# Splitting the gate matmuls of a fused LSTM and mixture-of-experts kernel: f, g and i first, o of both halves last

## The chip, the cores and the metric

The kernel runs on one core of one Trainium2 chip. The metric is the device time of one execution in microseconds (us). The time before is the median of three runs, 2253.83 us (2253.7 to 2257.63).

## What is computed

The input `x` has N = 2 sequences of T = 1024 steps with D = 256 features; all data are 32-bit floats. An LSTM with 256 units runs over the steps, from a given first hidden state and a zero cell state:

```python
def step(carry, xw_t):
    prev_h, prev_c = carry
    a = xw_t + prev_h @ Wh                   # Wh: 256 x 1024, xw = x @ Wx + b
    i = jax.nn.sigmoid(a[:, :Hdim])
    f = jax.nn.sigmoid(a[:, Hdim:2 * Hdim])
    o = jax.nn.sigmoid(a[:, 2 * Hdim:3 * Hdim])
    g = jnp.tanh(a[:, 3 * Hdim:])
    next_c = f * prev_c + i * g
    next_h = o * jnp.tanh(next_c)
    return ((next_h, next_c), next_h)
```

Its outputs are added to `x`. A mixture of experts follows on each token: two shared experts (SiLU-gated, 512 wide), and of eight routed experts (GELU, 256 wide) the two with the best scores, weighted by gates. Their scaled sum is added again.

## The kernel before

Each step needs the hidden state of the step before, so the 1,024 steps run one after the other (the loop over `t`). The experts of tokens that are done are cut into small units and put between the steps.

**The recurrent product.** The 256 units are kept as two halves `m` (K = 2), the 256 inputs of the product as two halves `k`. The stationary operand is a window of 32 columns of the stored hidden states (`h_window`): two of them hold the current step, the others are zero, so that eight steps (TH) of one group of gates can gather in the same PSUM tile, each in rows of its own. The moving operand is 64 columns of `wh_sb`: a pair of gates of 32 units. Four such products, `q` = 0 to 3, write the four groups of 32 PSUM partitions of `ps[m]`. `BLOCKS` lists the order of the eight blocks (k, m, pair) of four products in a step. The first three need only half 0 of h, the other five need half 1. A product of 32-bit floats is two weight loads and two matmuls in the profile (all on line 255, in `product`).

**The cell update.** For each half VectorE transposes `ps[m]` (128x64) in blocks of 32x32 within the same PSUM bank (line 787). ScalarE takes the sigmoids of i, f and o (line 790, 6 elements per partition) and the tanh of g (line 791, 2 elements). VectorE multiplies f by the old cell state (line 794), copies g into `seen` (line 798), and a scan over four elements (line 799) makes i * g + f * c for both sequences; its factors are zeros, which `results` fills beforehand by two ScalarE copies per 16 steps (line 697), and i. ScalarE takes the tanh of the cell state (line 807), VectorE multiplies by o and writes the new h (line 810). The order on VectorE is: both transposes; forget, copy and scan of half 0; the same of half 1; both h.

**Around it.** The products of `x` with `Wx` are made in blocks of 128 steps and kept with their bias by ScalarE (`keep_inputs`, line 613). `inject` puts them into the gate tile of the next eight steps by matmuls with the identity, at least one product per step. `Fill` holds queues of units of expert work for TensorE, ScalarE and VectorE; each step takes from them what its due time asks for, for TensorE at most two full products (ROOM), or, when nothing is due, one idle product with the identity.

The order of instructions is that of the program text. The code counts TensorE's instructions, four per product (`fill.issued`), and a table `WAITS` of steps with an additional one. Where the count would reach a multiple of 256 (FETCH) within the first 16 instructions (EARLY) of the next step, it injects one product more or cuts an injection into pieces:

```python
count = next(
    (n for n in range(max(0, t % TH + 1 - put), left + 1)
     if -(fill.issued + 4 * n) % FETCH > EARLY), left)
first = -(fill.issued + 4 * count) % FETCH
for i in range(count):
    more = i == count - 1 and first <= EARLY
    inject(nxt, t // TH + 1, put, 2 + first // 4 if more else 1)
    put += 1
```

Of the kernel before, what the change touches and what calls it, by code (L numbers as in the profile page):

```python
# [16 lines left out]
P = 128  # L17
N = 2
# [3 lines left out]
Q = 4  # L22
# [26 lines left out]
FETCH = 256  # L49
EARLY = 16  # L50
WAITS = (
    1, 8, 16, 24, 32, 40, 48, 56, 64, 72, 80, 88, 96, 104, 112, 120, 128, 136, 144, 149,
    152, 157, 160, 160, 165, 168, 176, 181, 184, 189, 192, 197, 200, 208, 216, 224, 232,
    240, 248, 256, 264, 272, 280, 288, 296, 304, 312, 320, 328, 336, 344, 352, 360, 368,
    376, 384, 392, 400, 408, 416, 419, 421, 423, 424, 428, 430, 432, 435, 437, 439, 440,
    440, 447, 448, 456, 464, 472, 480, 488, 496, 504, 512, 520, 528, 529, 536, 544, 552,
    560, 568, 576, 584, 592, 600, 608, 616, 624, 632, 640, 648, 656, 664, 672, 680, 688,
    688, 696, 704, 712, 720, 728, 736, 744, 752, 760, 768, 776, 784, 792, 800, 808, 816,
    824, 832, 840, 848, 856, 864, 872, 880, 888, 896, 904, 912, 920, 928, 930, 933, 935,
    936, 940, 942, 944, 947, 949, 951, 952, 956, 958, 960, 963, 965, 968, 976, 984, 992,  # L60
    999, 1000, 1004, 1006, 1008, 1011, 1013,
)
ISSUED = -188
# [4 lines left out]

BLOCKS = [
    (0, 0, 0), (0, 0, 1), (0, 1, 0), (1, 0, 0), (1, 0, 1), (0, 1, 1), (1, 1, 0), (1, 1, 1)  # L70
]


class Fill:
# [6 lines left out]
    def __init__(self):  # L81
        self.pe, self.act, self.dve = deque(), deque(), deque()
        self.aside = deque()
        self.last = False
        self.issued = ISSUED
        self.step = 0
        self.banks = FILL_BANKS
# [47 lines left out]
def lstm_moe_kernel(  # L135
# [89 lines left out]
    zero = const.tile([P, TB, K, N], F32, name="zero")  # L225
    nc.vector.memset(zero, 0.0)
# [20 lines left out]
    stepsp = ctx.enter_context(tc.tile_pool(name="steps", bufs=2))  # L247
# [5 lines left out]
    def product(*operands, **how):  # L253
        fill.issued += 4
        nc.tensor.matmul(*operands, **how)  # L255
# [348 lines left out]
    blocks = {}  # L604
    made = set()

    def pairs(blk):
        flat = blocks[blk].rearrange("p (h c) w -> p h (c w)", c=2)
        return flat.rearrange("p h (g c r) -> p h g c r", c=2, r=PAIR)

    def keep_inputs(blk, tile_, w0, w1, ps):
        h, c = divmod(tile_, 2)
        nc.scalar.activation(  # L613
            pairs(blk)[:, h, w0 // PAIR : w1 // PAIR, c, :],
            ps[:, : w1 - w0].rearrange("p (g r) -> p g r", r=PAIR),
            AF.Identity, bias=b_sb[:, tile_ : tile_ + 1],
        )
        made.update((blk, tile_, w) for w in range(w0, w1, PAIR))
# [12 lines left out]
    def queue_inputs(blk, w0=0):  # L631

        if w0 == 0:
            blocks[blk] = inputs.tile([P, 2 * Q, N * XB], F32, name="inputs")
        st = {}

        def unit(i, j):
            if j == 0:
                st["ps"] = bank()
            ps = st["ps"]  # L640
            input_product(blk, 2 * i + j // K, j % K, w0, N * XB, ps[:, j // K])
            if j == 2 * K - 1:
                fill.to_act(0.5, lambda: keep_inputs(blk, 2 * i, w0, N * XB, ps[:, 0]))
                fill.to_act(0.5, lambda: last(2 * i + 1, ps))

        def last(tile_, ps):
            keep_inputs(blk, tile_, w0, N * XB, ps[:, 1])
            fill.let_go()

        fill.pe.extend(  # L650
            (int(j == 0), 2, lambda i=i, j=j: unit(i, j)) for i in range(Q) for j in range(2 * K)
        )

    def inject(banks, grp, i, pieces=1):
        m, q = divmod(i, Q)
        blk, g = divmod(grp, XB // TH)
        assert all((blk, 4 * m + 2 * (q // 2) + c, g * PAIR) in made for c in range(2))
        for piece in range(pieces):
            w0, w1 = 64 * piece // pieces, 64 * (piece + 1) // pieces
            product(  # L660
                banks[m][0][q * ROWS : (q + 1) * ROWS, w0:w1],
                pairs(blk)[:, 2 * m + q // 2, g].rearrange("p c r -> p (c r)"),
                ident[:, q % 2 * 64 + w0 : q % 2 * 64 + w1],
                start=(piece == 0), stop=False, skip_group_check=True,
            )

    def gates_tile(m):

        a = gates_ps.tile([P, 4, P], F32, name=f"ps{m}")
        return a[:, 0, :64], a[:, 1, :64], a[:, 2:]  # L670
# [21 lines left out]
    def results():  # L692
        flat = stepsp.tile([P, TB, K, 8 * N], F32, name="results")
        sgm = flat[:, :, :, : 6 * N].rearrange("p u m (a n z) -> p u m a n z", n=N, z=2)
        gf = flat[:, :, :, 6 * N :].rearrange("p u m (n z) -> p u m n z", z=2)
        for m in range(K):
            nc.scalar.activation(sgm[:, :, m, 0, :, 0], zero[:, :, m], AF.Copy)
        return sgm, gf


    nc.scalar.activation(stepp.tile([P, N], F32, name="seen0"), zero[:, 0, 0], AF.Sigmoid)
    nxt_results = results()

    cells = [cells_ps.tile([P, 3, N, 2], F32, name=f"c{m}") for m in range(K)]
    c_prev = [cells[m][:, 1] for m in range(K)]
    for m in range(K):
        nc.vector.memset(cells[m], 0.0)
# [3 lines left out]
    nxt = [gates_tile(m) for m in range(K)]  # L711
# [6 lines left out]
    blocks[0] = inputs.tile([P, 2 * Q, N * XB], F32, name="inputs")  # L718
# [6 lines left out]
    for i in range(K * Q):  # L725
        inject(nxt, 0, i)
    due = 12
    for t in range(T):
        fill.step = t
        grp, u = divmod(t, TB)  # L730
        if t % TH == 0:
            cur, nxt = nxt, [gates_tile(m) for m in range(K)]
            ps, turned, busy = [a[0] for a in cur], [a[1] for a in cur], nxt[0][2]
            spare = False
        if u == 0:
            sgm, gf = nxt_results
# [9 lines left out]
        for k, m, pair in BLOCKS:  # L746
            for q in range(Q):
                w0 = q * D + m * P + pair * 64
                product(
                    ps[m][q * ROWS : (q + 1) * ROWS],  # L750
                    h_window(t, k, pair),
                    wh_sb[:, k, w0 : w0 + 64],
                    start=False,
                    stop=(t % TH == TH - 1 and k == K - 1 and pair == 1),
                    skip_group_check=True,
                )
        left = max(1, due - t)
        done = fill.run_pe(-(-len(fill.pe) // left), ROOM)
        if t % TH == 0:
            spare = not done  # L760
        if spare and not done:
            product(
                busy, ident, ident.unsqueeze(1).to_broadcast([P, 2, P]),
                start=(t % TH == 0), stop=False, skip_group_check=True,
            )

        if t // TH + 1 < T // TH:
            put = put if t % TH else 0
            fill.issued += WAITS.count(t)

            left = K * Q - put
            count = next(
                (n for n in range(max(0, t % TH + 1 - put), left + 1)
                 if -(fill.issued + 4 * n) % FETCH > EARLY), left)
            first = -(fill.issued + 4 * count) % FETCH
            for i in range(count):
                more = i == count - 1 and first <= EARLY
                inject(nxt, t // TH + 1, put, 2 + first // 4 if more else 1)
                put += 1

        rows = slice(N * (t % TH), N * (t % TH + 1))
        gates = [turned[m].rearrange("p (a r) -> p a r", r=PAIR)[:, :, rows] for m in range(K)]
        c_new = [cells[m][:, t % 2] for m in range(K)]
        seen = [stepp.tile([P, N], F32, name=f"seen{m}") for m in range(K)]
# [4 lines left out]
        def squash(m):  # L789
            nc.scalar.activation(sgm[:, u, m, :, :, 1], gates[m][:, 0:3], AF.Sigmoid)  # L790
            nc.scalar.activation(gf[:, u, m, :, 0], gates[m][:, 3], AF.Tanh)  # L791

        def forget(m):
            nc.vector.tensor_mul(gf[:, u, m, :, 1], sgm[:, u, m, 2, :, 1], c_prev[m][:, :, 1])  # L794

        def cell(m):

            nc.vector.tensor_copy(seen[m], gf[:, u, m, :, 0])  # L798
            nc.vector.tensor_tensor_scan(  # L799
                c_new[m].rearrange("p n z -> p (n z)"),  # L800
                sgm[:, u, m, 0].rearrange("p n z -> p (n z)"),
                gf[:, u, m].rearrange("p n z -> p (n z)"),
                0.0, ALU.mult, ALU.add,
            )

        def squash_cell(m):
            nc.scalar.activation(cells[m][:, 2, :, 0], c_new[m][:, :, 1], AF.Tanh)  # L807

        def output(m):
            nc.vector.tensor_mul(h_cols(t + 1)[:, m], sgm[:, u, m, 1, :, 1], cells[m][:, 2, :, 0])  # L810
# [4 lines left out]
        for m in range(K):  # L815
            forget(m)
            cell(m)
            squash_cell(m)
        for m in range(K):
            output(m)  # L820
        if u == TB // 2 and t + TB < T:
            nxt_results = results()
        else:
            fill.run(fill.act, 1.0)
        c_prev = c_new
# [102 lines left out]
```

## Time and profile before

| | |
|---|---|
| Runs: median, lowest, highest | 2253.83, 2253.7, 2257.63 us |
| Profiled execution, and its span | 2254.8 us, 2254.8 us |
| Granted TensorE clock, mean over the span | 0.996 |
| Busy: TensorE, its weight loads, VectorE, ScalarE | 2033.5, 1484.8, 1571.3, 909.5 us |
| Recurrent matmuls (line 255, 128x64) | 65536, mean 221 ns |
| Transposes (line 787) | 2048, mean 265 ns |
| Sigmoids of i, f, o (line 790) and tanh of g (line 791) | 2048 each, mean 176 and 167 ns |
| Forget product, copy, scan (lines 794, 798, 799) | 2048 each, mean 156, 162, 175 ns |
| Tanh of the cell (line 807), new h (line 810) | 2048 each, mean 157 and 153 ns |

PE is TensorE's matmul side, PEld its weight loads, DVE is VectorE, ACT ScalarE, SP the engine that issues most DMAs. Matmul records overlap, so the busy time of PE is no measure of how much of the array works. In a timeline the columns are start, duration, engine, line, operation, result <- operands, shape and number of instructions merged; in brackets stands the engine's idle time before, and what ended it. "issue" there means that the engine waited for nothing that the profile shows.

### The profile page before, as it was taken

The numbers are of one execution on the slowest core, as the hardware profiler recorded it, in microseconds if no ns is written. First come the engines' busy times: TensorE is split into PE (matmuls) and PEld (weight loads), VectorE is DVE, ScalarE is ACT, GpSimd is POOL, SyncE is SP. The second block draws the span as 40 slices with busy tenths as digits, with TensorE's granted clock in tenths as the row PEclk, the third lists the DMA queues.
The fourth block names the chain that finished last, engine by engine and source line by source line (L and its number), as shares of the span: only waits on it lengthen the run. The fifth ranks groups of instructions, "written<-read, shape, count | busy, mean of one in ns | idle before, by whom it ended". The sixth has DMA issues, their size and how long they took to land.

```text
span 2254.8 us, 159246 instructions
## 1 busy us (share of the span) xinstructions
PE 2033.5 (90%) x70612; PEld 1484.8 (66%) x70612; DVE 1571.3 (70%) x11041; ACT 909.5 (40%) x6487; POOL 2.7 (0%) x9
## 2 busy tenths in 40 slices
PE   8988899888989889998798899988898988989998
PEld 6666666666666666777666666666666666667787
DVE  5666667776777667777667767676676776667776
ACT  3334344433444334443344443444434344334443
POOL 0000000000000000000000000000000000000000
PEclk9999999999999999999999999999999999999999
DMA  2111100000000000000000000000000000000000
GB/s 65 35 35 35 35 28 5 5 5 7 7 5 5 5 7 7 5 7 7 5 6 5 5 5 7 7 4 5 5 7 7 4 5 5 7 7 5 5 9 7
DMA packets 15330, 23.84 MB, mean 11 GB/s; under 512 B 2864, under 2 KB 14128, under 8 KB 14640
## 3 DMA queue, kind: packets, MB, share of 16 engines
q1 hardware_dynamic: 14352, 12.62, 1.9%
q8 instruction: 552, 9.04, 1.7%
q14 instruction: 138, 1.13, 0.2%
q10 hardware_dynamic: 288, 1.05, 0.1%
HBM read 11.56 MB, written 2.10 MB: 6 GB/s over the span
## 4 chain that ended last, share of the span: by engine, by line
PE 61%; DVE 36%; issue 3%; DMA 0%; SPq 0%; ACT 0%
PE ps L255 53%; DVE ps L787 10%; DVE c L799 10%; PE ps_f L255 8%; DVE results L794 7%; DVE seen L798 6%; DVE h L810 3%; DMA wh_sb<-in_wh_dram 0%; SPq L165 0%; DVE acc L534 0%; SPq L173 0%; SPq L171 0%; SPq L170 0%; DVE acc L492 0%; ACT y L542 0%
## 5 line engine op out<-in xcount | busy, mean ns | idle before, releaser
L255 PE MATMUL ps<-wh_sb,h 128*32 128x64 f32 x65536 | 1143.8, 221 | 214.3 <-DVE h L810 210.5
L255 PEld LDWEIGHTS ps<-wh_sb,h 128*32 128x32 f32 x65536 | 975.1, 110 | 393.1 <-DVE h L810 386.8
L787 DVE STREAM_TRANSPOSE ps<-ps 128x64 f32<-128x64 f32 x2048 | 543.4, 265 | 498.5 <-PE ps L255 426.0
L790 ACT ACTIVATE results<-ps 128x6 f32<-128x6 f32 x2048 | 361.3, 176 | 1103.8 <-DVE ps L787 1009.4
L810 DVE TENSOR_TENSOR h<-results,c 128x2 f32<-128x2 f32 x2048 | 314.2, 153 | 168.4 <-ACT c L807 168.2
L807 ACT ACTIVATE c<-c 128x2 f32<-128x2 f32 x2048 | 321.5, 157 | 217.5 <-DVE c L799 181.7
L799 DVE TENSOR_TENSOR_SCAN c<-results 128x4 f32<-128x4 f32 x2048 | 358.2, 175 | 0.0
L791 ACT ACTIVATE results<-ps 128x2 f32<-128x2 f32 x2048 | 342.4, 167 | 0.0
L798 DVE COPY seen<-results 128x2 f32<-128x2 f32 x2048 | 332.8, 162 | 0.0
L794 DVE TENSOR_TENSOR results<-results,c 128x2 f32<-128x2 f32 x2048 | 319.3, 156 | 0.0
L255 PEld LDWEIGHTS ps<-ident,inputs 128*32 128x32 f32 x2090 | 124.0, 108 | 265.7 <-issue 228.4
L255 PE MATMUL ps<-ident,inputs 128*32 128x64 f32 (+2 forms) x2090 | 263.9, 230 | 0.3
L255 PE MATMUL ps_f<-x2T,w_sb 128*128 128x256 f32 (+3 forms) x640 | 173.4, 379 | 0.0
L255 PE MATMUL ps_f<-x2T,r_sb 128*128 128x256 f32 (+3 forms) x640 | 173.2, 378 | 0.0
L255 PE MATMUL ps_f<-r_sb,h_r 128*128 128x256 f32 (+1 forms) x520 | 165.9, 419 | 0.9 <-DVE acc L492 0.9
L255 PEld LDWEIGHTS ps_f<-x2T,r_sb 128*128 128x128 f32 (+1 forms) x640 | 88.5, 184 | 22.8
L255 PEld LDWEIGHTS ps_f<-x2T,w_sb 128*128 128x128 f32 (+1 forms) x640 | 86.7, 184 | 21.8 <-issue 0.2
L255 PEld LDWEIGHTS ps_f<-r_sb,h_r 128*128 128x128 f32 (+1 forms) x520 | 80.0, 184 | 23.3 <-DVE acc L492 1.3
L255 PE MATMUL ps_f<-xT_sb,wx_sb 128*128 128x256 f32 (+2 forms) x384 | 84.5, 346 | 0.3 <-ACT inputs L613 0.3
L255 PE MATMUL ps<-ident 128*128 128x256 f32 x232 | 82.8, 443 | 1.4 <-POOL ident masks.py:199 1.4
L255 PE MATMUL ps_f<-w_sb,h_s 128*128 128x256 f32 (+1 forms) x256 | 82.6, 419 | 0.0
L492 DVE SCALAR_TENSOR_TENSOR acc<-ps_f,gate,acc 128x256 f32<-128x256 f32 (+1 forms) x128 | 61.1, 478 | 1.2 <-PE ps_f L255 1.0
(87 smaller groups left out, 475.1 us busy)
## 6 DMA issues: line engine op xcount, KB each, us to landing
r_sb<-in_r_w1T_dram SPq DMA_DIRECT2D x16, 128.0 KB, 2.5
r_sb<-in_r_w2T_dram SPq DMA_DIRECT2D x16, 128.0 KB, 2.1
out_dram<-acc SPq DMA_DIRECT2D x15, 128.0 KB, 2.1
xT_sb<-in_xT_dram SPq DMA_DIRECT2D x14, 128.0 KB, 2.5
wx_sb<-in_wx_dram ACTq DMA_DIRECT2D x2, 512.0 KB, 4.3
wh_sb<-in_wh_dram SPq DMA_DIRECT2D x2, 512.0 KB, 6.2
w_sb<-in_s_w1T_dram SPq DMA_DIRECT2D x8, 128.0 KB, 2.2
w_sb<-in_s_w3T_dram SPq DMA_DIRECT2D x8, 128.0 KB, 2.2
```

The costliest lines, as they stand in the source:

```text
L255: nc.tensor.matmul(*operands, **how)
L492: nc.vector.scalar_tensor_tensor(acc, ps, st["gate"][:, i, e : e + 1], acc, ALU.mult, ALU.add)
L787: nc.vector.transpose(turned[m], ps[m])
L790: nc.scalar.activation(sgm[:, u, m, :, :, 1], gates[m][:, 0:3], AF.Sigmoid)
L791: nc.scalar.activation(gf[:, u, m, :, 0], gates[m][:, 3], AF.Tanh)
L794: nc.vector.tensor_mul(gf[:, u, m, :, 1], sgm[:, u, m, 2, :, 1], c_prev[m][:, :, 1])
L798: nc.vector.tensor_copy(seen[m], gf[:, u, m, :, 0])
L799: nc.vector.tensor_tensor_scan(c_new[m].rearrange("p n z -> p (n z)"), sgm[:, u, m, 0].rearrange("p n z -> p (n z)"), gf[:, u, m].rearrang ...
L807: nc.scalar.activation(cells[m][:, 2, :, 0], c_new[m][:, :, 1], AF.Tanh)
L810: nc.vector.tensor_mul(h_cols(t + 1)[:, m], sgm[:, u, m, 1, :, 1], cells[m][:, 2, :, 0])
```

## The change

The four gates get a new order in the weights, f, g, i, o, and each half's products are cut differently. Per half and input half there are now three kinds of blocks: f and g together (64 columns), i alone (32 columns) and o alone (32 columns). The o blocks of both halves go last and into one tile of its own, `out_gate`, in another PSUM bank; it is reused by every group of eight steps. A step has 12 blocks of four products instead of eight.

```diff
+FG, IN, OUT = (0, 0, 64), (1, 64, 96), (None, 96, 128)
 BLOCKS = [
-    (0, 0, 0), (0, 0, 1), (0, 1, 0), (1, 0, 0), (1, 0, 1), (0, 1, 1), (1, 1, 0), (1, 1, 1)
+    (0, 0, FG), (0, 0, IN), (0, 1, IN),
+    (1, 0, FG), (1, 0, IN), (0, 1, FG), (1, 1, FG), (1, 1, IN),
+    (0, 0, OUT), (0, 1, OUT), (1, 0, OUT), (1, 1, OUT),
 ]
+ORDER = [1, 3, 0, 2]
+PUT = [0, 0, 2, 4, 5, 6, 7, 8, 8]
...
-        for k, m, pair in BLOCKS:
+        for i, (k, m, (pair, a, b)) in enumerate(BLOCKS):
+            into = ps[K if pair is None else m]
             for q in range(Q):
-                w0 = q * D + m * P + pair * 64
+                w0 = q * D + m * P
                 product(
-                    ps[m][q * ROWS : (q + 1) * ROWS],
-                    h_window(t, k, pair),
-                    wh_sb[:, k, w0 : w0 + 64],
+                    into[q * ROWS : (q + 1) * ROWS, : b - a],
+                    h_window(t, k, m if pair is None else pair),
+                    wh_sb[:, k, w0 + a : w0 + b],
```

The sigmoid is taken as a tanh of half the argument: the weights, inputs and bias of g are doubled once (on the chip), one tanh with a scale of 0.5 covers f, g and i of a half, and the missing (1 + ...) / 2 are put into the forget product and the scan. The scan has eight elements, four per sequence, with constants set once; the copies into `seen` and the fills of `results` go. The o gates of both halves get one 128x32 transpose and one sigmoid.

```diff
         def squash(m):
-            nc.scalar.activation(sgm[:, u, m, :, :, 1], gates[m][:, 0:3], AF.Sigmoid)
-            nc.scalar.activation(gf[:, u, m, :, 0], gates[m][:, 3], AF.Tanh)
+            at = bass.AP(
+                tensor=res.tensor,
+                offset=res[:, t % SLOTS, m, 0:1].offset,
+                ap=[res.ap[0], [9, 3], [4, N]],
+            )
+            nc.scalar.activation(at, gates[m][:, 0:3], AF.Tanh, scale=0.5)
+
+        def squash_out():
+            nc.scalar.activation(into[:, :, 0:N, 1], gates[K], AF.Sigmoid)

         def forget(m):
-            nc.vector.tensor_mul(gf[:, u, m, :, 1], sgm[:, u, m, 2, :, 1], c_prev[m][:, :, 1])
+            nc.vector.scalar_tensor_tensor(
+                into[:, m, N : 2 * N, 2], into[:, m, 0:N, 0], 1.0, c_old[m][:, :, 3],
+                ALU.add, ALU.mult,
+            )

         def cell(m):
-            nc.vector.tensor_copy(seen[m], gf[:, u, m, :, 0])
             nc.vector.tensor_tensor_scan(
                 c_new[m].rearrange("p n z -> p (n z)"),
-                sgm[:, u, m, 0].rearrange("p n z -> p (n z)"),
-                gf[:, u, m].rearrange("p n z -> p (n z)"),
-                0.0, ALU.mult, ALU.add,
+                own[:, m, 2], own[:, m, 1], 0.0, ALU.mult, ALU.add,
             )
...
-        for m in range(K):
-            forget(m)
-            cell(m)
-            squash_cell(m)
+        forget(0)
+        transpose(K)
+        squash_out()
+        cell(0)
+        squash_cell(0)
+        forget(1)
+        cell(1)
+        squash_cell(1)
         for m in range(K):
             output(m)
-        if u == TB // 2 and t + TB < T:
-            nxt_results = results()
-        else:
-            fill.run(fill.act, 1.0)
-        c_prev = c_new
+        if t % TH == TH - 1 and t + 1 < T:
+            for q in range(Q):
+                inject(nxt, t // TH + 1, K * Q + q)
+        if t % TH == 3:
+            nc.scalar.activation(stepp.tile([P, N], F32, name="seen"), outs[0], AF.Copy)
+        fill.run(fill.act, 1.0)
```

The injections of f, g and i follow the fixed list `PUT`, without a count of TensorE's instructions: `FETCH`, `EARLY`, `WAITS` and the pieces are gone. The four injections of o come at the end of each eighth step. The kept inputs of o have a tile of their own, so a pair of input tiles takes three ScalarE passes instead of two. The next pair of gate tiles is opened one step later than before.

```diff
         if t // TH + 1 < T // TH:
-            put = put if t % TH else 0
-            fill.issued += WAITS.count(t)
...
-                inject(nxt, t // TH + 1, put, 2 + first // 4 if more else 1)
-                put += 1
+            for i in range(PUT[t % TH], PUT[t % TH + 1]):
+                inject(nxt, t // TH + 1, i)
```

## The prediction, made before the changed kernel ran

> **What bounds the kernel now.** I read the head of the page, its DMA queues and its chain of waits first, then the timeline of one step engine by engine, then TensorE's weight loads around a stall.
>
> ```profile
> span 2254.8 us, 159246 instructions
> PE 2033.5 (90%) x70612; PEld 1484.8 (66%) x70612; DVE 1571.3 (70%) x11041; ACT 909.5 (40%) x6487; POOL 2.7 (0%) x9
> ...
> q8 instruction: 552, 9.04, 1.7%
> ...
> PE 61%; DVE 36%; issue 3%; DMA 0%; SPq 0%; ACT 0%
> ```
>
> The 90% of PE does not mean a full array: a matmul record lasts about 220 ns and overlaps its neighbours. The 70,612 matmul and 70,612 weight-load records are what I need later. The timeline of one step (start, duration, instruction, count; VectorE lines, then ScalarE lines) shows a ring of dependencies:
>
> ```profile
> 1001.16 0.16 DVE L810 TENSOR_TENSOR h<-results,c 128x2 f32<-128x2 f32 x1 [0.16 <-ACT c L807]
> ...
> 1001.89 0.60 DVE L787 STREAM_TRANSPOSE ps<-ps 128x64 f32<-128x64 f32 x2 [0.17 <-PE ps L255]
> ...
> 1002.73 0.16 DVE L794 TENSOR_TENSOR results<-results,c 128x2 f32<-128x2 f32 x1
> 1002.80 0.16 DVE L798 COPY seen<-results 128x2 f32<-128x2 f32 x1
> 1002.92 0.17 DVE L799 TENSOR_TENSOR_SCAN c<-results 128x4 f32<-128x4 f32 x1
> ...
> 1003.32 0.16 DVE L810 TENSOR_TENSOR h<-results,c 128x2 f32<-128x2 f32 x1 [0.17 <-ACT c L807]
> ```
>
> ```profile
> 1002.18 0.18 ACT L790 ACTIVATE results<-ps 128x6 f32<-128x6 f32 x1 [1.05 <-DVE ps L787]
> ...
> 1002.52 0.18 ACT L790 ACTIVATE results<-ps 128x6 f32<-128x6 f32 x1
> ...
> 1003.13 0.16 ACT L807 ACTIVATE c<-c 128x2 f32<-128x2 f32 x1 [0.18 <-DVE c L799]
> ```
>
> The second h of a step (1001.16) releases the matmuls that need it; the second transpose follows 1.06 us later, its gates' sigmoid 0.30 after that, the forget product 0.21, the scan 0.19, the tanh 0.21, the next h 0.19: 2.16 us. Over all 1,023 steps the median from h to h is 2.154 us, with no, one or two filling products alike. 1,023 x 2.154 = 2203.5, plus 11.6 us to the first such h and 20.8 us after the last, is 2236; the other 18.7 us are steps that run over, nearly all of them between h and the second transpose, in TensorE's part.
>
> Most of those overruns have one look. TensorE's weight loads:
>
> ```profile
> 1095.93 0.14 PEld L255 LDWEIGHTS ps<-ident,inputs 128*32 128x32 f32 x3 [0.26 <-issue]
> 1096.29 0.94 PEld L255 LDWEIGHTS ps<-wh_sb,h 128*32 128x32 f32 x64 [0.22 <-DVE h L810]
> 1097.32 0.30 PEld L255 LDWEIGHTS ps_f<-x2T,r_sb 128*128 128x128 f32 x2
> 1098.44 0.92 PEld L255 LDWEIGHTS ps<-wh_sb,h 128*32 128x32 f32 x59 [0.83 <-DVE h L810]
> 1099.67 0.15 PEld L255 LDWEIGHTS ps<-wh_sb,h 128*32 128x32 f32 x5 [0.31 <-issue]
> ```
>
> TensorE stops at 1095.93 and again at 1099.67 with "issue" as the cause, waiting for no engine. Between the stops lie 3+64+2+59 = 128 weight loads, and as many matmuls: 256 instructions. 552 instruction packets of 16 KB (9.04 MB) for 141,224 records is also one packet per 256. With the records counted in order of start, every break of over 100 ns inside a burst of these matmuls stands on the same count modulo 256. So **a new packet of 256 instructions gates TensorE**. Between two gates exactly one packet is moved, and in the packet records no gate opens sooner than about 1.24 us after the last packet has landed: whenever TensorE would have arrived earlier, it stopped until 1.2 to 1.5 us were over; whenever later, it ran through.
>
> **The price of a packet.** At this count TensorE stopped for 60 ns or more 37 times; in these (medians) the next packet starts 1.14 us after the gate, takes 1.06, and the next gate opens 1.43 after it landed: 3.64 us. Where two gates in a row were stopped, they lie 3.56, 3.75 and 3.74 us apart (the last is the one shown). I take 3.65 us per 256 instructions; the intervals that end in a stop reach from 3.16 to 4.45, four of them are under 3.3. Today 256 instructions fill 1.85 steps, 4.0 us, so the gate is mostly open in time: 552 x 3.65 = 2015 of 2254.8 us. The kernel stands 10% away from a second limit that no share of busy time shows.
>
> **The change, part by part.** Times of a step below count from the second h.
>
> *TensorE's work on the ring.* The ring waits for rounds of four matmuls, one per 32 columns. A 64-wide round takes 55.6 ns by successive starts; a 32-wide one 31.7 ns (the prologue's input products have this shape, seven rounds in a row). Every matmul is two rounds. From h to the second transpose the old order has five blocks, 10 x 55.6 = 556 ns; the new one three 64-wide and two 32-wide, 6 x 55.6 + 4 x 31.7 = 460, and its last matmul lasts 196 instead of 219 ns: 119 ns less. The blocks that need only the first h shrink from 334 to 238 ns, off the ring, since the second h is awaited behind them. The output gates' four blocks, 254 ns, are new behind the ring's part; their transpose could start at 1.19 us, beside the forget product at 1.16.
>
> [...]
>
> *VectorE and ScalarE.* The two copies (162 ns) and the separate tanh of g (167 ns) lie beside the ring: a scan starts 192 ns after its forget product, which is that product's 156 plus 36, so nothing comes earlier without the copy. The forget product with an added 1 is a three-operand form; the router's 128x2 row of that form lasts 155 ns: no change. The scan of 8 is not in the trace: between nothing and another 175 ns (twice the scan of 4); I take 10, as the scan of 4 is only 19 ns over a 2-wide product. The 128x32 transpose is not there either: between a 2-wide product's 155 and the 265 of 128x64. It stands in VectorE's queue before the first scan; if the output matmuls are late, both scans and the second forget product are late behind it. One sigmoid for both output gates replaces the two tanhs. The constant fills of the results (22 us on ScalarE) go, 128 small copies and a third copy of inputs per two tiles come: ScalarE is 40% busy and covers them; uncovered they are about 30 us. Four output injections per eight steps go in front of the next step's matmuls, before h arrives, inside TensorE's wait for it. Prologue: VectorE scales weights and biases after their load, about 1 us.
>
> Sum of the ring: 2.154 - 0.119 + 0.010 = 2.045 us.
>
> *TensorE's instructions.* 32 matmuls per step become 48. The built program holds 52,159 matmuls against 35,306, and each is four instructions (35,306 x 4 = 141,224, the two x70612 of the page). So 208,636 instructions: **815 packets instead of 552**, 204 instructions per step. At a ring of 2.045 us, 256 of them would pass in 2.57 us, far under 3.65; even from the end of one burst to the head of the next but one, the longest way, it is two steps less some 0.7 us, 3.3. So every gate is reached too early, and the packets set the pace: 3.65 x 204 / 256 = 2.91 us per step. What the ring gains is then hidden. The old placing of gates by split injections is dropped too; with every gate late it could not have helped.
>
> Sum: the first gate at 7.35 us plus 1 for the prologue; the 20.8 us tail holds 326 matmul records, 652 instructions or 2.5 packets; the 815 - 1 - 2.5 = 811 others x 3.65 = 2960. 8.4 + 2960 + 20.8 = 2989. I predict **2990 us**, against the profiled execution's 2254.8 (the median of the runs shown is 2253.83, 0.04% less, so no correction). With 3.30 us per packet, about the shortest stops, it is 2705; with 3.85 (the packets of 1.3 us that also occur in place of 1.06) 3152.
>
> [...]
>
> **Rivals.**
> 1. *The ring still decides; faster.* If more packets can be under way once they are asked for faster, the gate never closes: 11.6 + 1 + 1,023 x 2.045 + 18.7 + 20.8 = 2144 us. For it: most gates pass without a stop today. Against: in no case did a gate open early after a landing, and one packet, never two, came between gates. It decides from 2.6 us per packet down.
> 2. *Half hidden.* The 1.14 us from gate to packet may shrink, as they are about 0.5 after some gates that were passed without a stop. 3.65 - 0.64 = 3.01 us per packet gives 2470; from 2260 up to 2700 I count here. For it: a packet's own time varies, 0.88 to 1.6 us; against: after a stop the wait for the next packet was never under 0.7.
> 3. *The clock falls as well.* TensorE's array would work (0.95 + 0.43 us for one filling product) / 2.91 = 47% of the time. Steps 12 to 15 have no filling product (0.89 / 2.154 = 41%), and from 40.1 to 50.3 us the granted clock was 0.50; steps there took 0.67 to 0.88 us more. Added to 2.045 this is about 2.8 us, still under 2.91, so mostly hidden; where it isn't, up to 0.25 us per step, 3250.
>
> **How the numbers follow.** Forecast 0.81 (2705 to 3152), the first rival 0.09, the second 0.05, the third beyond the range 0.05. The range is the forecast's own, rounded to 2700 to 3160; what lies beyond it on both sides is 2 in 10 at most. About 0.2% is what a measurement of this kernel can tell from no change. Faster by more than that is the first rival but for a bad ring, 0.08; within it 0.01; slower 0.91.
>
> **What would show it.** About 815 instruction packets, some 3.6 us apart throughout; stops with "issue" as their cause in most steps, wherever the 256th instruction falls; h to h about 2.9 us on average; VectorE and ScalarE idle more than now. The ring's gain would show in steps without a gate: second transpose about 0.94 us after h. I am wrong if packets come closer than 3 us, or if stops fall elsewhere than every 256 instructions.

## The result, and the profile after

| | before | after |
|---|---|---|
| Runs: median, lowest, highest, us | 2255.73, 2253.7, 2260.43 (4 runs) | 3049.0, 3044.82, 3062.17 (4 runs) |
| Ratio, 95% interval | | 1.3518, [1.3483, 1.3553] |
| Profiled execution, its span, us | 2254.8, 2254.8 | 3044.82, 3043.0 |
| Granted TensorE clock, mean | 0.996 | 0.978 |

The changed kernel takes 35% longer. The head of its page, its instruction queue and its chain of waits answer to the first lines shown of before:

```profile
span 3043.0 us, 224493 instructions
PE 2297.4 (75%) x104318; PEld 1750.0 (58%) x104318; DVE 1622.1 (53%) x10025; ACT 893.3 (29%) x5500; POOL 3.9 (0%) x13
...
q8 instruction: 815, 13.35, 1.9%
...
PE 71%; issue 23%; DVE 5%; ACT 0%; DMA 0%; SPq 0%
```

TensorE does 48% more instructions (104,318 records on each side against 70,612), yet its busy share falls from 90% to 75%. VectorE's share falls too, 70% to 53%. No engine took over; every one is idler. What grew in the chain is "issue", from 3% to 23% of the span, which is time in which nothing that the profile records was being waited for, and the number of instruction packets, from 552 to 815.

The view of all waits (engine, tile, line, what was waited for: us in total, times, longest) of the kernel after gives the size:

```profile
DVE ps L808 <- PE ps L246: 924.6, 1149, 3.4
PEld ps L246 <- issue: 671.1, 1113, 1.8
...
PEld ps_o L246 <- issue: 304.9, 251, 1.7
```

Before, TensorE's weight loads for the gate tiles stopped for "issue" 704 times, 233.0 us in total and 0.7 us at the longest; most of that is a pause of 0.33 us in front of a step's injection (one stands at 1004.74 below), and at the gates TensorE stopped only 37 times, for 9 us. Now it is 671.1 us for the gate tiles, and 304.9 more for the new tile of o, with stops of up to 1.8 us. VectorE's 924.6 us of waiting for the gate matmuls is largely the same time seen from the other end.

Where the stops fall can be counted. TensorE's weight loads in the kernel after, over 4 us (start, duration, instruction, number merged, and in brackets the idle time before and what ended it):

```profile
1003.73 0.33 PEld L246 LDWEIGHTS ps_o<-wh_sb,h 128*32 128x32 f32 x28 [0.96 <-issue]
1004.11 0.30 PEld L246 LDWEIGHTS ps_f<-w_sb,h_s 128*128 128x128 f32 x2
1004.74 0.14 PEld L246 LDWEIGHTS ps<-ident,inputs 128*32 128x32 f32 x4 [0.33 <-issue]
1004.99 0.80 PEld L246 LDWEIGHTS ps<-wh_sb,h 128*32 128x32 f32 x64
1005.68 0.39 PEld L246 LDWEIGHTS ps_o<-wh_sb,h 128*32 128x32 f32 x30
1007.75 0.14 PEld L246 LDWEIGHTS ps_o<-wh_sb,h 128*32 128x32 f32 x2 [1.69 <-issue]
```

Between the stops at 1003.73 and 1007.75 lie 28+2+4+64+30 = 128 weight loads; with their matmuls these are 256 instructions, in 4.02 us. (The gate before was stopped at 1000.26, and the 3.47 us up to 1003.73 hold 128 loads as well.) The last stop falls near the end of the o products, after 30 of their 32 loads. What that does to the cell update is seen on VectorE, in the same step:

```profile
1005.68 0.55 DVE L808 STREAM_TRANSPOSE ps<-ps 128x64 f32<-128x64 f32 x2 [0.51 <-PE ps L246]
1006.19 0.16 DVE L822 SCALAR_TENSOR_TENSOR results<-results,ps 128x2 f32<-128x2 f32 x1
1008.04 0.23 DVE L808 STREAM_TRANSPOSE ps_o<-ps_o 128x32 f32<-128x32 f32 x1 [1.69 <-PE ps_o L246]
1008.18 0.14 DVE L829 TENSOR_TENSOR_SCAN ps<-results 128x8 f32<-128x8 f32 x1
```

The gates f, g and i were transposed by 1006.23, and the first forget product was done at 1006.35. Its scan, and the forget product and scan of half 1 after it, then stand 1.69 us behind the transpose of o in VectorE's queue. In other steps the gate falls into the products of f, g and i, and the first transposes are late instead (924.6 us of waits against 302.5 for the transpose of o).

Over the whole execution, gate to gate is 3.71 us on the mean (median 3.745), 780 of the 815 gates stopped TensorE for 60 ns or more (from the start of one record to that of the next), 845 us in all, and from h to h it is 2.938 us on the mean. Breaks of over 100 ns within the weight loads of one tile, with "issue" as their cause, occur 703 times, and all of them stand on the same count modulo 256, to within one instruction. The 810 steps with a gate inside take 3.146 us on the mean, the 213 without one 2.061 (median; 2.146 on the mean).

### The profile page after: what moved, and what is told of

Read it like the earlier page. It is cut to its first block, busy times and chain, and to the rows that moved or that the text cites. A ratio compares the mean times of both kernels' runs of the same rounds, so it can differ in the third digit from the quotient of the medians.

```text
span 3043.0 us, 224493 instructions
## 1 busy us (share of the span) xinstructions
PE 2297.4 (75%) x104318; PEld 1750.0 (58%) x104318; DVE 1622.1 (53%) x10025; ACT 893.3 (29%) x5500; POOL 3.9 (0%) x13
## 4 chain that ended last, share of the span: by engine, by line
PE 71%; issue 23%; DVE 5%; ACT 0%; DMA 0%; SPq 0%
PE ps L246 40%; PE ps_f L246 19%; PE ps_o L246 12%; DVE ps L808 2%; DVE ps_o L808 1%; DVE c L829 1%; DVE results L822 1%; DVE h L838 1%; DVE ps L829 0%; DMA wh_sb<-in_wh_dram 0%; ACT results L819 0%; ACT c L835 0%; ACT inputs L619 0%; ACT L819 0%; SPq L156 0%
## 5 line engine op out<-in xcount | busy, mean ns | idle before, releaser
L246 PE MATMUL ps<-wh_sb,h 128*32 128x32 f32 (+1 forms) x65536 | 1099.1, 213 | 428.4 <-issue 378.5
L808 DVE STREAM_TRANSPOSE ps<-ps 128x64 f32<-128x64 f32 x2048 | 543.2, 265 | 951.8 <-PE ps L246 924.6
L246 PE MATMUL ps_o<-wh_sb,h 128*32 128x32 f32 x32768 | 568.5, 200 | 277.3 <-issue 277.2
L246 PEld LDWEIGHTS ps_o<-wh_sb,h 128*32 128x32 f32 x32768 | 455.4, 112 | 302.9 <-issue 302.6
L808 DVE STREAM_TRANSPOSE ps_o<-ps_o 128x32 f32<-128x32 f32 x1024 | 234.1, 229 | 305.3 <-PE ps_o L246 302.5
L819 ACT ACTIVATE results<-ps_o 128x4 f32<-128x4 f32 x1024 | 181.7, 177 | 408.9 <-DVE ps L829 347.2
L246 PE MATMUL ps<-ident,inputs 128*32 128x64 f32 x2048 | 234.8, 234 | 4.5 <-issue 4.1
L829 DVE TENSOR_TENSOR_SCAN c<-results 128x8 f32<-128x8 f32 x1024 | 186.4, 182 | 35.5
L835 ACT ACTIVATE c<-c 128x2 f32<-128x2 f32 x1024 | 160.8, 157 | 112.2
L835 ACT ACTIVATE squashed<-ps 128x2 f32<-128x2 f32 x1024 | 173.7, 170 | 0.0
L838 DVE TENSOR_TENSOR h<-results,squashed 128x2 f32<-128x2 f32 x1024 | 164.4, 161 | 1.1 <-ACT squashed L835 1.1
```

What stands on the lines that cost most here:

```text
L808: nc.vector.transpose(turned[m], ps[m])
L819: nc.scalar.activation(into[:, :, 0:N, 1], gates[K], AF.Sigmoid)
L829: nc.vector.tensor_tensor_scan(c_new[m].rearrange("p n z -> p (n z)"), own[:, m, 2], own[:, m, 1], 0.0, ALU.mult, ALU.add,)
L835: nc.scalar.activation(outs[m], c_new[m][:, :, 3], AF.Tanh)
L838: nc.vector.tensor_mul(h_cols(t + 1)[:, m], into[:, m, 0:N, 1], outs[m])
```

## The experiments

The theory to test was that the packets of 256 TensorE instructions set the pace, 3.7 us each. The rivals were that something else in the change (late o, the new cell update, the new order) costs the time, and that the gate would give way when asked for faster. The measured columns of all runs, with packets, median of h to h over the 1,023 steps, and stops of 60 ns or more at a gate:

| run | time, us | ratio to before, 95% | packets | h to h, us | stops |
|---|---|---|---|---|---|
| before | 2255.73 | | 552 | 2.154 | 37 |
| after | 3049.0 | 1.3518 [1.3483, 1.3553] | 815 | mean 2.938 | 780 |
| pad16 | 2998.08 (one run) | | 808 | mean 2.897 | 761 |
| pad4 | 2333.13 | 1.0357 [1.0328, 1.0386] | 616 | 2.154, mean 2.244 | 244 |
| no_out | 2197.07 (one run) | | 559 | 2.061 | 109 |
| stream | 944.28 (one run) | | 256 (its page counts 255) | | 255 |
| wide | 2509.15 | 1.1126 [1.1107, 1.1144] | 551 | 2.383 | 28 |
| wide2 | 2274.55 | 1.0097 [1.008, 1.0114] | 551 | 2.175 | 32 |
| merged | 2276.57 | 1.0106 [1.0089, 1.0123] | 559 | 2.179 | 44 |
| merged2 | 2219.03 | 0.9832 [0.9819, 0.9846] | 559 | 2.108 | 77 |

The kernel before took 2254 to 2257 us (medians) beside these runs. In wide, wide2, merged and no_out breaks of 60 ns also stand one count beside the gate, 11 to 29 times each, so as many of their stops need not be gates; in before these are 2 and 4.

### pad16: before, with as many instructions as after

Sixteen small products, 2 columns wide, follow the recurrent products of each step in the kernel before; nothing else is changed. Although they write a corner that no instruction reads, pad16 and pad4 don't compute the LSTM's result; why was not looked into, and only their time is used here.

```diff
+        for i in range(16):
+            product(
+                busy[i % Q * ROWS : (i % Q + 1) * ROWS, 1, -2:], ident[:, :ROWS], ident[:, :2],
+                start=True, stop=True, skip_group_check=True,
+            )
         left = max(1, due - t)
```

Expected:

> The kernel before with 16 more products per step, each of 32 columns by 2, into a corner of PSUM that nothing reads, put behind the step's recurrent products where TensorE waits anyway. The ring of dependencies is untouched; TensorE's instructions rise from 141,224 to 206,760 (808 packets of 256). Packet gate: 3.7 us per packet as measured in the changed kernel, about 3000 us. If the ring decides and packets are hidden: 2255 to 2300 us, as the small products take some 0.3 us in a wait of 1.1 us.

Measured: 2998.08 us. The head, the instruction queue and the chain of the page of pad16:

```profile
span 2995.9 us, 224827 instructions
...
q8 instruction: 808, 13.24, 1.8%
...
PE 76%; issue 19%; DVE 5%; DMA 0%; SPq 0%; ACT 0%
```

This is the profile of the changed kernel without any of its cell update, order or cut. Its weight loads stop by the same count:

```profile
1502.26 0.54 PEld L255 LDWEIGHTS ps<-wh_sb,h 128*32 128x32 f32 x35 [0.18 <-issue]
1502.69 0.11 PEld L255 LDWEIGHTS ps<-ident 128*32 128x32 f32 x1
1502.73 0.12 PEld L255 LDWEIGHTS ps<-wh_sb,h 128*32 128x32 f32 x3
1502.75 0.44 PEld L255 LDWEIGHTS ps<-ident 128*32 128x32 f32 x31
1503.21 0.41 PEld L255 LDWEIGHTS ps_f<-ident_s,x2T 128*64 128x64 f32 x4
1503.59 0.25 PEld L255 LDWEIGHTS ps_f<-w_sb,h_s 128*64 128x64 f32 x2
1504.22 0.81 PEld L255 LDWEIGHTS ps<-wh_sb,h 128*32 128x32 f32 x52 [0.39 <-DVE h L815]
1506.00 0.20 PEld L255 LDWEIGHTS ps<-wh_sb,h 128*32 128x32 f32 x10 [0.97 <-issue]
```

Between the stops at 1502.26 and 1506.00 us lie 35+1+3+31+4+2+52 = 128 of them, in 3.74 us. The sixteen products take 0.44 us of a step in weight-load records. Even if none of that fell into a wait, it would be 450 us in 1,024 steps, but they cost 744 us. 761 of the 808 gates stopped TensorE, 720 us in all. The rival in which only the ring counts is refuted: by it this kernel would be about as fast as before.

### pad4: the same with four

```diff
-        for i in range(16):
+        for i in range(4):
```

Expected:

> The same with 4 more products per step: 157,608 instructions, 616 packets, 256 instructions per 1.66 steps = 3.58 us of the ring, just under the gate's 3.7. Packet gate: 616 x 3.7 + 25 = about 2300 us, 2% slower than before. If the ring decides: 2255 to 2265 us.

Measured: 2333.13 us, 3.6% above before. The median step keeps its 2.154 us, and 244 gates stop, for 101 us in all. 616 packets at 3.7 us are about 2280, or 2300 with start and tail, so here neither limit alone gives the time. The stops at the gates are 92 us more than the 9 us of before, and the run is 79 us longer than before beside it (2254.43). So with 256 instructions in 3.58 us of the ring, single stops already cover what the kernel lost, and it lost more than the simple product says.

### stream: the gate by itself

Only products 32 wide and 2 columns long, one after the other, without any wait for another engine; what the kernel computes is left out.

```diff
+COUNT = 16384
...
+    for i in range(COUNT):
+        r = i % Q * ROWS
+        nc.tensor.matmul(
+            ps[r : r + ROWS, :2], ident[:, :ROWS], ident[:, :2],
+            start=(i < Q), stop=(i >= COUNT - Q), skip_group_check=True,
+        )
...
```

Expected:

> The disputed price by itself. Everything but the output's shape is left out (it is filled with zeros and a corner of a product): 16,384 products of 32 columns by 2, in the four column groups in turn, waiting for nothing: 65,536 instructions, 256 packets. Packet gate: 256 x 3.7 = about 950 us, with one stop per 256 instructions. If TensorE's own issue decides (about 7 ns per instruction in a burst of the kernel before): about 460 us. If packets can be moved one behind the other (1.1 us each): about 290 to 460 us.

Measured: 944.28 us for 65,536 TensorE instructions. The weight loads:

```profile
500.24 1.80 PEld L154 LDWEIGHTS ps<-ident 128*32 128x32 f32 x128 [1.67 <-issue]
503.98 1.80 PEld L154 LDWEIGHTS ps<-ident 128*32 128x32 f32 x128 [1.94 <-issue]
507.73 1.80 PEld L154 LDWEIGHTS ps<-ident 128*32 128x32 f32 x128 [1.94 <-issue]
```

TensorE works for 1.80 us on a packet, then stands for 1.83 us on the mean (1.67 in half of the stops, 1.9 or more in nearly all others), so that gates lie 3.63 us apart. Between these products stands no wait for a semaphore or another engine, and the kernel's output is moved only after 930 us. From gate to the packet's start it is 1.14 us, the packet takes 1.04, and the gate opens 1.39 after it landed (medians): the same three parts as in the kernel before (1.14, 1.06 and 1.43), where they were read from 37 stops.

### no_out: the split without the instructions of o

The recurrent products of the o gates are left out of the kernel after (its output lacks them); transposes, sigmoid, scans and order stay.

```diff
-    (0, 0, OUT), (0, 1, OUT), (1, 0, OUT), (1, 1, OUT),
```

Expected:

> The changed kernel without the recurrent products of the o gates (their inputs and bias stay, so the output differs): the ring's other parts, the 32-column products of i and all of the new cell update stay; 32 products per step again, 559 packets. Packet gate: the step falls to the ring's 2.05 us with some stops left, 2140 to 2210 us in all. If the split products, the small transpose or the new cell update themselves make the step long: 2600 us or more.

Measured: 2197.07 us, with 559 packets, and 2.061 us from h to h (median; 2.109 on the mean, with the 109 stops). VectorE in one step:

```profile
1000.35 0.16 DVE L837 TENSOR_TENSOR h<-results,c 128x2 f32<-128x2 f32 x1
...
1001.53 0.16 DVE L821 SCALAR_TENSOR_TENSOR results<-results,ps 128x2 f32<-128x2 f32 x1
1001.60 0.22 DVE L807 STREAM_TRANSPOSE ps_o<-ps_o 128x32 f32<-128x32 f32 x1
1001.74 0.17 DVE L828 TENSOR_TENSOR_SCAN ps<-results 128x8 f32<-128x8 f32 x1
...
1002.41 0.16 DVE L837 TENSOR_TENSOR h<-results,c 128x2 f32<-128x2 f32 x1
```

From the second h of one step to that of the next 2.06 us: the shorter way through TensorE is real, 0.09 us per step, and the transpose of o (0.22 us) fits between the first forget product and its scan. So the ring of the change was faster, as intended; the 16 products more per step made it irrelevant. A kernel that keeps all its work with this cut has the 815 packets of after, and took 3049 us.

### wide: the new cell update with the old cut

Three edits to the kernel after: blocks of 64 columns again (f with g, i with o), no tile of o's own, and one sigmoid per half.

```diff
-FG, IN, OUT = (0, 0, 64), (1, 64, 96), (None, 96, 128)
+FG, IN = (0, 0, 64), (1, 64, 128)
...
         def squash_out():
-            nc.scalar.activation(into[:, :, 0:N, 1], gates[K], AF.Sigmoid)
+            for m in range(K):
+                nc.scalar.activation(into[:, m, 0:N, 1], gates[m][:, 3], AF.Sigmoid)
...
         forget(0)
-        transpose(K)
...
```

Expected:

> The new cell update and gate order with the old cut of the products: eight blocks of 64 columns (f with g, i with o), o transposed with the others, one sigmoid per half. About 551 packets. Packet gate: the step is the old ring's 2.154 us (the update is worth nothing on it) plus stops that are no longer avoided: 2255 to 2310 us. If the cell update costs time: over 2310; if the copies and the second tanh had been on the ring: under 2200.

Measured: 2509.15 us, far above that. The packets are not the cause, 551 with 28 stops. The waits of wide have a line that no other kernel has, on VectorE:

```profile
DVE ps L829 <- ACT results L819: 248.2, 1024, 1.7
```

and VectorE's timeline shows it in each step:

```profile
1002.16 0.16 DVE L822 SCALAR_TENSOR_TENSOR results<-results,ps 128x2 f32<-128x2 f32 x1
1002.55 0.18 DVE L829 TENSOR_TENSOR_SCAN ps<-results 128x8 f32<-128x8 f32 x1 [0.24 <-ACT results L819]
```

ScalarE beside it:

```profile
1002.35 0.23 ACT L819 ACTIVATE results<-ps 128x2 f32<-128x2 f32 x2
```

The scan of half 0 writes its cell state into the gate tile (`ps<-results`), of which the two sigmoids of o (line 819, from 1002.35 to 1002.58 on ScalarE) read another part. In the kernel after, o lies in a tile of its own. The scan waits until these sigmoids are done, 0.24 us on the mean in every one of 1,024 steps: 248.2 us, against 255 measured beyond before. It is a cost of this experiment's edit, not of the gate.

### wide2: the same, with the cell state elsewhere

```diff
...
-        new = states(cur[0][3])[:, (t + 1) % 2]
+        new = states(out_gate[:, 0])[:, (t + 1) % 2]
...
```

(The first state and its zeroing move with it.)

Expected:

> As wide, but with the cell state of half 0 in a tile that no transposed gates share, so that the scan of half 0 has no reason to wait for the sigmoids of o, as it did in wide (0.24 us per step). Packet gate and old ring: 551 packets, step 2.15 to 2.17 us, 2250 to 2310 us. If the new cell update itself is slow in this place: it stays near 2500 us.

Measured: 2274.55 us, 2.175 us from h to h. The wait is gone, and with it 235 us. What remains are the new cell update (scan of 8, no copies, one tanh for three gates), the order and the fixed injections, with the old width of the products and the old number of packets: 0.8 to 1.1% slower than before. No gain from the copies and the tanh of g that it saves is to be seen, which fits the lines of before, where they lie beside the ring. The 0.02 us that the step got longer was not split among the other parts.

### merged: after's idea without more instructions

Instead of cutting i and o to 32 columns for each half, i of both halves makes one product of 64 columns, and o of both halves another. A step has eight blocks again.

```diff
+FG0, IN, FG1, OUT = (0, 0, 0), (0, 1, 64), (1, 0, 128), (2, 1, 192)
+BLOCKS = [
+    (0, FG0), (0, IN), (0, FG1), (1, FG0), (1, IN), (1, FG1), (0, OUT), (1, OUT)
+]
...
```

The transpose of o is 128x64; one tanh takes f, g and i of half 0 with i of half 1, another f and g of half 1; both forget products stand behind the transpose of o on VectorE.

Expected:

> The intent of the change with the old count of products: i of both halves in one product of 64 columns, o of both halves in one, so eight blocks of 64 columns and 559 packets; f, g of each half and i first (six blocks), o last in its own bank with one 128x64 transpose; one tanh for f, i, g of half 0 and i of half 1, one for f, g of half 1; the new scan. Ring: three blocks of 111 ns from h to the second transpose in place of five, 2.154 - 0.223 + up to 0.07 for the queue on VectorE = 1.93 to 2.0 us. Packet gate: 256 instructions in 1.85 steps, so not under 3.7 / 1.85 = 2.0 us a step on average: 2100 to 2170 us, faster than both kernels. If the gate did not matter: 2020 to 2085 us. If a ring with o last is slower than the sum says: over 2200 us.

Measured: 2276.57 us, 2.179 from h to h, a miss against the 2100 to 2170 expected: the packets stayed at 559 as meant, but the ring was no shorter. VectorE of merged, around h:

```profile
1400.90 0.16 DVE L824 TENSOR_TENSOR h<-results,squashed 128x2 f32<-128x2 f32 x1
1401.00 0.16 DVE L824 TENSOR_TENSOR h<-results,c 128x2 f32<-128x2 f32 x1
1401.94 0.40 DVE L796 STREAM_TRANSPOSE ps<-ps 128x64 f32<-128x64 f32 x2 [0.79 <-PE ps L245]
```

The two h are 0.10 us apart. The three blocks that need only the first h take 0.334 us, so they no longer fit ahead of the second h; and nearly all six blocks of f, g and i (12 rounds x 55.6 ns = 667 ns) lie on the ring, where before has five.

### merged2: the halves staggered again

```diff
-    (0, FG0), (0, IN), (0, FG1), (1, FG0), (1, IN), (1, FG1), (0, OUT), (1, OUT)
+    (0, FG0), (0, IN), (1, FG0), (1, IN), (0, FG1), (1, FG1), (0, OUT), (1, OUT)
...
+        forget(0)
         transpose(K)
         squash_out()
-        for fn in (forget, cell, squash_cell):
-            for m in range(K):
-                fn(m)
+        cell(0)
+        squash_cell(0)
+        forget(1)
+        cell(1)
+        squash_cell(1)
```

Expected:

> merged with another order and nothing else: the products that transpose 0 needs come first from both input halves (f, g of half 0 and i from the first h, the same from the second h), then f, g of half 1 from both; VectorE's order is the changed kernel's (forget 0, transpose of o, scan 0, forget 1, scan 1). In merged the two h of a step lay 0.1 us apart, so all six blocks, 667 ns, stood on the ring (2.179 us). Here transpose 1 follows transpose 0 by two blocks, 222 ns, so the second h comes about 222 ns after the first and hides the two blocks before it: four blocks, 445 ns, on the ring, 2.06 us, and up to 0.06 more where the transpose of o pushes the second forget product. 559 packets set no less than 2.0 us a step. Forecast 2150 to 2230 us, under the kernel before. If the two h stay close together whatever the order: 2270 us again.

Measured: 2219.03 us, ratio 0.9832 with an interval of 0.9819 to 0.9846: 1.7% faster than before. Its runs took 2216 to 2224 us, those of the kernel before beside them 2253 to 2260, so it beats both kernels. VectorE of merged2 in one step:

```profile
1400.87 0.16 DVE L824 TENSOR_TENSOR h<-results,squashed 128x2 f32<-128x2 f32 x1
1401.12 0.16 DVE L824 TENSOR_TENSOR h<-results,c 128x2 f32<-128x2 f32 x1
1401.83 0.49 DVE L796 STREAM_TRANSPOSE ps<-ps 128x64 f32<-128x64 f32 x2 [0.55 <-PE ps L245]
...
1402.42 0.26 DVE L796 STREAM_TRANSPOSE ps_o<-ps_o 128x64 f32<-128x64 f32 x1
1402.59 0.14 DVE L814 TENSOR_TENSOR_SCAN ps<-results 128x8 f32<-128x8 f32 x1
```

The h are 0.25 us apart again, and the step takes 2.11 us where before has 2.154. The order of the products and that of VectorE changed together, so which of them set the h apart was not separated. The step lies 0.05 us above the ring of after and no_out: the second transpose comes 0.93 us after h here, 0.95 there, but behind the transpose of o (0.26 us instead of 0.22) and the first scan the second forget product starts at 1.52 us instead of 1.47 (medians).

## Why the prediction was right, step by step

*The packet count* was exact: 815.

*What bounds the kernel* was shown twice without any part of the change: pad16 adds only instructions to the kernel before and lands at 2998 us with 808 packets, and stream, which has nothing but instructions, needs 944 us for 256. From these two and after, 944 / 256 = 3.69, 2998 / 808 = 3.71, 3049 / 815 = 3.74 us per packet (whole times, starts and tails included); from gate to gate alone they are 3.63, 3.69 and 3.71. The signs of being wrong did not come: the mean interval stayed well over 3 us, and the stops stood where the 256th instruction falls. "Every gate is reached too early" was nearly so, 780 of 815. (Two steps less 0.7 us are 3.39, not the 3.3 of the prediction, which changes nothing as both are under 3.65.)

*The price of a packet* was the one term of size that was off: 3.65 us forecast from 37 stops, 3.71 measured over 815. The gap from gate to packet was 1.14 us as before, the packet took 1.11 instead of 1.06, and the gate opened 1.38 after landing instead of 1.43 (medians), together 3.63. The means are 1.20, 1.12 and 1.38, together 3.71, mostly because some packets start late, up to 2.3 us after their gate. The forecast had added medians, but over 811 packets means count: 811 x 0.06 = 49 us of the 56 that separate the forecast (2989) from the profiled execution. The prediction also named only three of the six pairs of successive stops that the trace of before has by its rule of 60 ns; the others lie 4.29, 4.45 and 5.35 us apart, so the pairs were a weaker support for 3.65 than they looked.

*The prologue* was the second: 1 us forecast, an estimate for VectorE's scaling that no row of before gives; in after it takes 0.29 us twice for `wh_sb` and 0.57 for the bias. The first gate, with which the sum begins, came at 10.9 us (before at 7.35), 2.5 us later than forecast; the first second h came at 16.8 us, before at 11.6. VectorE scales the bias after the load of `wh_sb`, and ScalarE's first inputs wait for the bias; then ScalarE loads a table. ScalarE's timeline of after, two lines:

```profile
9.95 0.38 ACT L619 ACTIVATE inputs<-ps_f,b_sb,twice 128x32 f32<-128x32 f32 x1 [6.79 <-DVE b_sb L731]
...
15.13 1.28 ACT L819 ACT_TABLE_LOAD   x1
```

The first kept inputs of before start at 6.68 us. The later start here and the 1.28 us for the table were not in the sum. They are small against 3045 us.

*The ring* was forecast at 2.045 us and is 2.061 (medians), both in the 213 steps of after without a gate and in no_out. The second transposes stand 0.95 us after h in both (0.94 forecast). The scan of 8 that is on the ring, of half 1, takes 182 ns against 175 for 4, so the 10 ns taken for it were near. The 128x32 transpose takes 229 ns, inside the bounds given. That this gain of 0.09 us per step would be hidden, as the prediction said, is what 3049 against no_out's 2197 us shows.

*The 32-wide rounds.* The forecast of the ring took 31.7 ns for them, from the prologue of before. Had they been as slow as the 64-wide ones (55.6 ns), the ring would have kept its 556 ns of rounds and stayed at 2.15 us; no_out's 2.06 speaks against that, and in the recurrent products of after the median is 31 to 33 ns. Narrow rounds are not always that short, though: those of stream, 2 columns long, follow one another every 54 ns, those of pad16 every 33 (median), and no run here shows why.

*One packet at a time.* Packets of 256 instructions agree with every count above. In stream 1.83 us of each 3.63 are a stop between one packet's instructions and the next, and in 812 of the 814 intervals of after exactly one packet is moved between two gates.

*The rivals.* The first (the ring decides, 2144 us) and the second (the gate gives way under load) fall with after, pad16 and stream: the gap from a gate that stopped TensorE to the packet's start was 1.14 us (median) in before, after and stream alike, whether 37 of 552 gates stopped it or all 255. The third (the clock falls as well) came in part: in the kernel after the granted clock was 0.50 for 133 us of the span, but the packet intervals there are 3.84 us against 3.71 overall, 51 of 814, so some 7 us. The gate at the end of these intervals still stopped TensorE for 60 ns or more in 30 of the 51, so much of the slower clock was hidden, as said.

*What was not separated.* Late o holds up both scans when a gate falls into it, but since pad16 loses nearly as much (744 us against 793) with no o to be late, that queueing is where the wait shows and not its cause. Moving the transpose of o behind the scans was not tried.

## What to carry to other kernels

Count TensorE's instructions per stage, not only its array time: here a product of 32-bit floats was four (52,159 products, 208,636 instructions) and every 256 were one packet (815). Every run that would have used 256 of them in less than about 3.7 us lost time at the gates: stream, pad16, after and pad4 took 3.69, 3.71, 3.74 and 3.79 us per packet of their whole time; at 3.9 us per packet single stops still took 2% (no_out, 44.6 us). So cutting a product into narrower ones, to have the urgent part sooner, paid here only while the number of instructions stayed under that limit; merge other pieces for each that is cut, as merged2 does (559 packets, 2219.03 us). And before building on a shorter chain in a recurrence that is kept in two halves, look at the gap between their results: merged lost all its gain (2.179 us from h to h) as the two came 0.10 us apart.

## What the runs showed of the hardware that was not expected

- TensorE alone spent 1.80 us on 256 instructions and then stood for 1.83 us on the mean, 255 times in a row (stream); a limit of 3.6 to 3.7 us per packet held from 256 packets in 944 us to 815 in 3049, with other engines at work or none.
- The instruction queue appears with 1.9% of the transfer engines' time in the page of after and bounds the kernel all the same: what counted here was the 3.71 us from gate to gate with one packet moved between them, not that share.
- A scan of eight elements takes 182 ns where one of four takes 175 (that of half 0, which writes into the gate tile, has 154 on the mean in after), and a ScalarE function of six elements 176 to 181 ns where one of two took 157 to 170: that scan aside, two or three times the elements cost 6 to 24 ns in these rows, where every instruction lasts over 150.
